# Down stages: normalized rows split in row form on GpSimd and turned by two-byte DMA transposes, in place of TensorE transposes

## The chip, the cores and the metric

The kernel runs on one core of a Trainium2 chip. The time is the device time of one execution in microseconds (us). A core has five engines that run side by side, each with an instruction queue of its own that is worked off in order: TensorE (PE in the profile, its weight loads PEld), VectorE (DVE), ScalarE (ACT), GpSimd (POOL) and SyncE (SP), which here only issues DMA transfers. An instruction starts when the one before it on its engine is through and the semaphores that it waits for are there. Matmul results go to PSUM, eight banks of 128 x 512 fp32; GpSimd doesn't read PSUM in this kernel.

## The reference, cut to what matters

The program is a macaron layer on x of 2048 tokens x 1024 features: half a feed-forward network, a state-space convolution, and half a feed-forward network again, with the same weights, each on the layer-normalized x.

```
x = x + 0.5 * ffn(layernorm(x))
x = x + s4(layernorm(x))          # convolution along the last axis
x = x + 0.5 * ffn(layernorm(x))

ffn(x): h = silu(x @ Wg) * (x @ Wu);  return h @ Wd
Wg, Wu: 1024 x 2752, Wd: 2752 x 1024
W[k, n] = (nibble(k, n) - (zero(group k, n) + 1)) * scale(group k, n)   # 4 bits, groups of 128 rows
```

All data is fp32. The change concerns `layernorm(x)` on its way into `x @ Wg` and `x @ Wu`.

## The kernel before

**Jobs.** The tokens are cut in four blocks of 512 (TB), each of four row tiles of 128 tokens (NT = 4). A feed-forward network for one block is a job, so there are eight; the list `JOBS` (L1351) gives block and kind (1: first network, 3: second). Each job has two stages. `gate_up` (the up stage, L669) runs over 64 steps: eight waves of output columns times eight groups of 128 input features. `down` (the down stage, L747) runs over 44 steps: two halves of the output features times 22 chunks of the hidden features. The last chunk of a half holds half as many matmuls.

**Precision.** The quantized weights are held as signed bytes in DRAM, and every step loads one tile of them (`load_bytes`, four steps ahead, on SP's DMA queue) and casts it to fp32r, a rounded fp32 (`make_weights`, three steps ahead, on GpSimd, L643). The other operand is split into two parts so that their sum is fp32: for the up stage xTh in fp32r and xTl, the rest, in fp16; for the down stage hh and hl (L727, L729, both made by GpSimd from hf). So each step of the down stage is 4 output chunks x 2 parts = 8 matmuls of 128 x 512. After each step ScalarE or VectorE multiplies the PSUM bank in place by a ratio of scales (L665, L667). The cast weights have five buffers (`wpool`), the bytes six (`bpool`). The cast of a step's weights therefore waits until TensorE is through with the step five before it.

**The normalized input.** The up stage needs the normalized rows transposed: features on the partitions, tokens along the free axis. xTh and xTl have one buffer each. They are free once the up stage of a job is through, and must be full when the up stage of the next job begins. So they are filled during the down stage between, while TensorE works on the down matmuls. This is done by hooks: `at(dn, step, f)` has f's instructions written at that step. For each row tile t of the next job's block (`ab`):

- at step 1 + 4t `normalized` (L218) subtracts the mean and multiplies by the reciprocal deviation on VectorE, 128 x 1024 at once (xn);
- at steps 2 + 4t and 4 + 4t `turn` (L234) handles one half of the 1024 features: four TensorE transposes of 128 x 128 into one PSUM bank (pt, L228), ScalarE's copy of it into xTh, which rounds to fp32r (L250), and VectorE's subtraction pt - xTh into xTl (L251).

Job 0's down stage is later (it starts at step 10) and takes another way with `by_pool=True`: ScalarE copies the bank to SBUF and GpSimd makes both parts (L246 to L248).

Down stages also reload x of the job's own block (`load_x`) and add the finished first output half back to it: four transposes of y per row tile (`back`, pb, L780), from step 26 on.

**Order.** A planner turns the written order into each engine's queue. It moves an instruction ahead of an earlier written one on the same engine if it takes the earlier one to be still waiting. Pools hand out buffers: `xpool` ten of 128 x 1024 fp32 (x, xn and other temporaries, by `t4`), `hfpool` and `gpool` three each of 128 x 512 fp32 (hf; silu's result g).

Of the kernel before, what the change touches and what calls it, by code (L numbers as in the profile page):

```python
# [9 lines left out]
F32 = mybir.dt.float32  # L10
BF16 = mybir.dt.bfloat16
F16 = mybir.dt.float16
# [4 lines left out]
F32R = mybir.dt.float32r  # L17
AF = mybir.ActivationFunctionType
ALU = mybir.AluOpType
# [5 lines left out]
P = 128  # L25
HID = 1024
INTER = 2752
TOK = 2048
TB = 512
NT = TB // P  # L30
NC = HID // P
# [24 lines left out]
def macaron_s4_kernel(  # L56
# [31 lines left out]
    nc = tc.nc  # L88
# [7 lines left out]
    xtpool = ctx.enter_context(tc.tile_pool(name="xT", bufs=1))  # L96
# [4 lines left out]
    gpool = ctx.enter_context(tc.tile_pool(name="g", bufs=3))  # L101
    hfpool = ctx.enter_context(tc.tile_pool(name="hf", bufs=3))
# [27 lines left out]
    def t4(name):  # L130
        return xpool.tile([P, HID], F32, tag="x", name=name)
# [9 lines left out]
    def in_order_of_writing(f, *engines):  # L141

        start = len(nc.cur_bb.bb.instructions)
        got = f()
        written = list(nc.cur_bb.bb.instructions)
        for e in engines:
            last = next((i for i in reversed(written[:start]) if i.engine == e), None)
            for ins in written[start:]:
                if ins.engine == e:
                    if last is not None:  # L150
                        tc.add_manual_dep(
                            ins,
                            last.name,
                            mybir.DependencyInfo(
                                mybir.DependencyClass.NoSync, mybir.DependencyReason.DATA
                            ),
                            reason="order of writing",
                        )
                    last = ins
        return got  # L160


    x = {}
    ln = {}

    def load_x(b, src):
        x[b] = []
        for t in range(NT):
            xt = t4(f"x_{b}_{t}")
            nc.sync.dma_start(xt, src[t])  # L170
            x[b].append(xt)

    def rows_of(dram, b):
        return [dram[bass.ds(b * TB + t * P, P), :] for t in range(NT)]

    def moments(b, k):
        for _ in moments_by_tile(b, k):
            pass

    def moments_by_tile(b, k):  # L180

        name = f"{b}_{k}"
        stats = small.tile([P, NT, 2, 6], F32, tag="stats", name=f"stats_{name}")
        mv = small.tile([P, NT, 2], F32, tag="mv", name=f"mv_{name}")
        for t in range(NT):
            for i in range(2):
                nc.vector.bn_stats(stats[:, t, i, :], x[b][t][:, bass.ts(i, 512)])  # L187
            nc.vector.bn_aggr(mv[:, t, :], stats[:, t, :, :].rearrange("p a s -> p (a s)"))
            yield
        guess(b, k, mv)  # L190
# [13 lines left out]
    def deviations(b, k, factor=1.0):  # L204


        mv, ve, r = ln.pop(b)
        e = small.tile([P, NT], F32, tag="e", name=f"e_{b}_{k}")
        for three in (3.0, 12.0, 768.0):
            nc.vector.tensor_tensor(e, r, r, ALU.mult)  # L210
            nc.vector.tensor_tensor(e, e, ve, ALU.mult)
            nc.vector.scalar_tensor_tensor(r, e, three, r, ALU.subtract, ALU.mult)
        nc.vector.tensor_scalar(r, r, -factor / 8192, None, ALU.mult)
        for t in range(NT):
            ln[b, t] = (mv[:, t, 0:1], r[:, t : t + 1], k)
        return r

    def normalized(b, t):  # L218
        m, r, k = ln[b, t]
        n = t4(f"xn_{b}_{k}_{t}")  # L220
        nc.vector.tensor_scalar(n, x[b][t], m, r, ALU.subtract, ALU.mult)
        return n

    def turned(n, name):

        ps = bank(name)
        for k in range(4):
            nc.tensor.transpose(ps[:, bass.ts(k, P)], n[:, bass.ts(k, P)], ident)  # L228
        return ps.rearrange("p (c t) -> p c t", c=4)


    pieces = {}

    def turn(b, t, n, half, by_pool=False):  # L234
        k = ln[b, t][2]
        if b not in pieces:
            pieces[b] = [
                xtpool.tile([P, NC, TB], dt, tag=f"xT{w}", name=f"xT{w}_{b}_{k}")
                for w, dt in (("h", F32R), ("l", F16))
            ]  # L240
        hi, lo = (a[:, 4 * half : 4 * half + 4, bass.ts(t, P)] for a in pieces[b])
        ps = turned(n, f"pt_{b}_{k}_{t}_{half}")
        if by_pool:
            both = gpool.tile([P, TB], F32, tag="g", name=f"turn_{b}_{k}_{t}_{half}")
            both = both.rearrange("p (c t) -> p c t", c=4)
            nc.scalar.copy(both, ps)  # L246
            nc.gpsimd.tensor_copy(hi, both)
            nc.gpsimd.tensor_tensor(lo, both, hi.bitcast(F32), ALU.subtract)  # L248
        else:
            nc.scalar.copy(hi, ps)  # L250
            nc.vector.tensor_tensor(lo, ps, hi.bitcast(F32), ALU.subtract)  # L251

# [275 lines left out]
    def in_pieces(at, hooks_and_steps, pieces):  # L530

        held = {}

        def piece(last):
            def step():
                if not held:
                    held[0] = pieces()
                for _ in held[0]:
                    if not last:
                        break  # L540

            in_order_of_writing(step, ET.DVE)

        for i, (hooks, s) in enumerate(hooks_and_steps):
            last = i == len(hooks_and_steps) - 1
            at(hooks, s, lambda last=last: piece(last))
# [114 lines left out]
    h = {}  # L661
# [128 lines left out]
    after = const.tile([P, 4, P], F32, tag="after", name="after")  # L790
# [227 lines left out]
    def s4_toeplitz():  # L1018

        rows, turn, whole = t4("s4_rows"), t4("s4_turn")[:, :P], t4("s4_whole")  # L1020
        nc.gpsimd.memset(turn, 0.0)
        nc.gpsimd.affine_select(
            out=turn,
            in_=turn,
            pattern=[[1, P]],
# [327 lines left out]
    def fast():  # L1353
        for j, (b, k) in enumerate(JOBS):
            prev = JOBS[j - 1] if j else None
            after = JOBS[j + 1] if j + 1 < len(JOBS) else None
            up, dn = {}, {}

            def at(hooks, s, f):
                hooks.setdefault(s, []).append(f)  # L1360
# [65 lines left out]
            if after:  # L1426
                ab, ak = after
                if ak == 1:
                    at(up, 55 if j == 0 else 6, lambda: load_x(ab, rows_of(u, ab)))
                    if j == 0:  # L1430
                        steps = [(dn, d) for d in range(3, 8)]
                        in_pieces(at, steps, lambda: moments_by_tile(ab, 1))
                        newton = lambda: deviations(ab, 1, LIFT)
                        at(dn, 8, lambda: in_order_of_writing(newton, ET.DVE))
                    else:
                        both = lambda: moments(ab, 1)
                        at(up, 44, lambda: in_order_of_writing(both, ET.DVE))
                        at(up, 45, lambda: deviations(ab, 1, LIFT))
                an = {}

                pool = j == 0

                def anorm(t):
                    an[t] = normalized(ab, t)

                o = 9 if j == 0 else 0
                for t in range(NT):
                    at(dn, o + 1 + 4 * t, lambda t=t: anorm(t))
                    at(dn, o + 2 + 4 * t, lambda t=t: turn(ab, t, an[t][:, :512], 0, by_pool=pool))
                    at(dn, o + 4 + 4 * t, lambda t=t: turn(ab, t, an[t][:, 512:], 1, by_pool=pool))  # L1450
# [6 lines left out]
        b = JOBS[-1][0]  # L1457
# [116 lines left out]
    srow_next, zeros_down = in_order_of_writing(start, *STARTING, ET.PE)  # L1574
    x.pop(0)
    fast()
    x.clear()
    other = nc.values_load(flag)
# [84 lines left out]
```

## Time and profile before

| what | us |
|---|---|
| median of 3 runs | 2136.39 (2135.84 to 2138.37) |
| the profiled execution | 2136.97 |
| its span, first to last instruction | 2135.1 |
| TensorE busy | 2087.0 |
| VectorE busy | 1702.1 |
| ScalarE busy | 1420.6 |
| GpSimd busy | 1072.9 |
| TensorE transposes pt (L228), 224, busy | 36.8 |
| ScalarE xTh <- pt (L250), 48 | 28.3 |
| VectorE xTl (L251), 48 | 33.1 |
| GpSimd weight casts for the down stages (L643), 352 | 222.4 |
| GpSimd waiting for TensorE before these | 338.6 |

The profile is of one execution. The span leaves out 1.9 us of its time before the first and after the last instruction. Busy times are sums over an engine's instructions. Those of TensorE overlap[...], so 128 x 128 transposes with a mean of 272 ns follow each other more closely than that; what a stretch of them takes is read from the chain in order of time. The chain is followed back from the last instruction, at each step to whatever released it. Of the 224 transposes pt 32 belong to job 0's down stage and 192 to those of jobs 1 to 6. The granted TensorE clock was 0.997 of full speed over the span.

### The profile page before, as it was taken

How to read it: one execution, taken by the hardware profiler on the slowest of the kernel's cores; microseconds unless marked ns; L12 is line 12 of the kernel's file. 1: busy time of each engine (PE TensorE's matmuls, PEld its weight loads, DVE VectorE, ACT ScalarE, POOL GpSimd, SP SyncE). 2: the span in 40 equal slices, each digit the busy share in tenths (PEclk: the TensorE clock that was granted, in tenths of full speed). 3: DMA queues.
4: the chain of work that ended last, by engine and by line, in shares of the span. 5: the costliest groups of instructions: out<-in, count | busy, mean ns of one | idle time of the engine just before them, and what ended most of it. 6: DMA issues, size and time to landing. Idle time of an engine off the chain costs nothing.

```text
span 2135.1 us, 30272 instructions
## 1 busy us (share of the span) xinstructions
PE 2087.0 (98%) x9748; PEld 1425.8 (67%) x9748; DVE 1702.1 (80%) x2781; ACT 1420.6 (67%) x2233; POOL 1072.9 (50%) x1438
## 2 busy tenths in 40 slices
PE   6999999999999999999999999999999999999997
PEld 4555665677776578665876568675686766866576
DVE  8988877778888777778777888878788787777776
ACT  6877777646655776676767766547775467767765
POOL 6867838743354643555335543455534545345632
PEclk9999999999999999999999999999999999999999
DMA  4434321112111211112121121112111131121111
GB/s 141 124 92 131 100 70 55 37 58 74 43 45 47 93 50 54 65 31 92 56 80 38 29 73 39 44 52 70 35 38 38 51 98 44 45 81 36 33 35 58
DMA packets 163110, 132.14 MB, mean 62 GB/s; under 512 B 22651, under 2 KB 150500, under 8 KB 162942
## 3 DMA queue, kind: packets, MB, share of 16 engines
q1 hardware_dynamic: 161926, 128.24, 19.7%
q8 instruction: 79, 1.29, 0.2%
q10 hardware_dynamic: 728, 1.29, 0.2%
q14 instruction: 89, 0.73, 0.1%
q0 software_dynamic: 288, 0.59, 0.1%
HBM read 104.45 MB, written 25.50 MB: 61 GB/s over the span
## 4 chain that ended last, share of the span: by engine, by line
PE 88%; DVE 6%; POOL 2%; DMA 1%; issue 1%; ACT 1%; SPq 0%; ACTq 0%; DVEq 0%; POOLq 0%
PE pg L695 53%; PE po L758 27%; PE pc L1084 3%; DVE pg L667 2%; PE pb L780 1%; PE pb L1084 1%; PE pt L228 1%; DVE po L667 1%; PE st L228 1%; DVE hf L725 1%; POOL q L551 0%; POOL qd L580 0%; POOL xTl L248 0%; DMA b<-wq 0%; POOL w_down L643 0%
## 5 line engine op out<-in xcount | busy, mean ns | idle before, releaser
L665 ACT ACTIVATE pg<-pg,rat 128x512 f32<-128x512 f32 x1240 | 787.1, 660 | 424.3 <-PE pg L695 423.2
L667 DVE TENSOR_TENSOR pg<-pg,rat 128x512 f32<-128x512 f32 x1168 | 776.9, 694 | 174.0 <-PE pg L695 170.0
L695 PE MATMUL pg<-xTh,w_up 128*128 128x512 f32 x2752 | 851.5, 438 | 2.7 <-DVE pg L667 1.7
L695 PE MATMUL pg<-xTl,w_up 128*128 128x512 f16 x2752 | 722.0, 382 | 8.5 <-POOL xTl L1518 3.2
L643 POOL CAST w_up<-b 128x768 fp32r<-128x768 int8 (+2 forms) x490 | 377.4, 776 | 519.0 <-PE pg L695 407.9
L695 PEld LDWEIGHTS pg<-xTh,w_up 128*128 128x128 f32 x2752 | 519.6, 189 | 176.8 <-DVE pg L667 14.9
L758 PE MATMUL po<-hl,w_down 128*128 128x512 f32 x1344 | 539.2, 403 | 9.5 <-DVE po L667 8.0
L665 ACT ACTIVATE po<-po,ratd 128x512 f32<-128x512 f32 x660 | 430.8, 662 | 159.0 <-PE po L758 159.0
L758 PE MATMUL po<-hh,w_down 128*128 128x512 f32 x1344 | 523.3, 392 | 0.0
L667 DVE TENSOR_TENSOR po<-po,ratd 128x512 f32<-128x512 f32 x620 | 427.4, 698 | 97.3 <-PE po L758 93.0
L695 PEld LDWEIGHTS <-w_up 128*128 128x128 bf16 x2752 | 228.1, 99 | 332.7 <-issue 156.2
L643 POOL CAST w_down<-bd 128x512 fp32r<-128x512 int8 x352 | 222.4, 634 | 410.2 <-PE po L758 338.6
L758 PEld LDWEIGHTS po<-hl,w_down 128*128 128x128 f32 x1344 | 251.9, 188 | 86.9 <-DVE po L667 21.9
L758 PEld LDWEIGHTS po<-hh,w_down 128*128 128x128 f32 x1344 | 252.8, 188 | 45.5
L729 POOL TENSOR_TENSOR hl<-hf,hh 128x512 fp32r<-128x512 f32 x168 | 220.1, 1310 | 7.9
L725 DVE SCALAR_TENSOR_TENSOR hf<-pg,rat,g 128x512 f32<-128x512 f32 x168 | 122.9, 748 | 45.5 <-ACT g L722 37.6
L722 ACT ACTIVATE g<-pg,rat 128x512 f32<-128x512 f32 x168 | 110.7, 687 | 49.2 <-PE pg L695 39.1
L727 POOL CAST hh<-hf 128x512 fp32r<-128x512 f32 x168 | 106.3, 633 | 55.5 <-PE pg L695 34.1
L187 DVE BATCH_NORM_STATS2 stats<-x 128x6 f32<-128x512 f32 x88 | 58.6, 677 | 0.5
L1114 DVE TENSOR_TENSOR x<-x,pc 128x512 f32<-128x512 f32 x32 | 22.0, 686 | 36.9 <-PE pc L1084 36.9
L1084 PEld LDWEIGHTS pc<-near,st 128*128 128x128 f32 x256 | 43.6, 190 | 7.9
L782 DVE TENSOR_TENSOR x<-x,pb 128x512 f32<-128x512 f32 x64 | 43.2, 679 | 6.2 <-PE pb L780 6.2
(210 smaller groups left out, 1049.7 us busy)
## 6 DMA issues: line engine op xcount, KB each, us to landing
b<-wq SPq DMA_DIRECT2D x319, 96.0 KB
bd<-wdq SPq DMA_DIRECT2D x336, 64.0 KB
x<-in_L_attn_u_dram SPq DMA_DIRECT2D x30, 512.0 KB
b<-wq SPq DMA_DIRECT2D x128, 64.0 KB
xs<-x SPq DMA_DIRECT2D x16, 512.0 KB
x<-xs SPq DMA_DIRECT2D x16, 512.0 KB
out_dram<-x SPq DMA_DIRECT2D x16, 512.0 KB
b<-wq SPq DMA_DIRECT2D x64, 80.0 KB
```

The costliest lines, as they stand in the source:

```text
L187: nc.vector.bn_stats(stats[:, t, i, :], x[b][t][:, bass.ts(i, 512)])
L643: nc.gpsimd.tensor_copy(t, b)
L665: nc.scalar.activation(dst, src, AF.Copy, scale=sc)
L667: nc.vector.tensor_tensor(dst, src, sc.to_broadcast([P, TB]), ALU.mult)
L695: nc.tensor.matmul(p, weights, (lo, hi)[k][:, g, :], start=(g == 0 and not done), stop=(g == GK - 1 and done), skip_group_check=True,)
L722: nc.scalar.activation(g, pg, AF.Silu, scale=rat[:, 2 * f, GK - 1 :])
L725: nc.vector.scalar_tensor_tensor(hf, pu, last, g, ALU.mult, ALU.mult)
L727: nc.gpsimd.tensor_copy(hi, hf)
L729: nc.gpsimd.tensor_tensor(lo, hf, hi.bitcast(F32), ALU.subtract)
L758: nc.tensor.matmul(ps[c], w[:, bass.ts(c, P)], part, start=(f == 0 and k == 0), stop=(f == NF - 1), skip_group_check=True,)
L782: nc.vector.tensor_tensor(part, part, ps, ALU.add)
L1084: nc.tensor.matmul(dst, lhsT, rhs, start=start, stop=stop, skip_group_check=True)
```

## The change

In the down stages of jobs 1 to 6 a new generator `turn_by_dma` takes the place of `turn`; job 0 keeps the old way, and job 7 has no job after it. Per row tile:

- VectorE normalizes in two halves of 512 columns.
- GpSimd makes, from the rows as they are, hi (xn rounded to fp32r), top (xn in bf16), mid = hi - top in bf16 and lo = xn - hi in fp16, each in two halves. top + mid stand for hi.
- SP issues three DMA transposes of 128 x 1024 two-byte elements: top and mid into one temporary (`both`, the tile named turned), lo directly into xTl.
- GpSimd adds the transposed top and mid into xTh, in two halves (`sums`).

The temporaries: xn, hi and turned are tiles of `xpool` (`t4`), top and mid of `hfpool`, lo of `gpool`. PSUM and TensorE have no part in it. The hooks advance the generator at steps 1 + 9t + d, with d = 0 for the normalization, 1 to 6 for GpSimd's pieces, 8 for the transposes, 10 and 11 for the sums. Lines behind the new function are 47 further down in the changed kernel, and 59 behind the second edit.

```diff
--- before.py
+++ after.py
@@ -249,6 +249,53 @@
         else:
             nc.scalar.copy(hi, ps)
             nc.vector.tensor_tensor(lo, ps, hi.bitcast(F32), ALU.subtract)
+
+    def turn_by_dma(b, t, after):
+
+
+
+        k = ln[b, t][2]
+        name = f"{b}_{k}_{t}"
+        if b not in pieces:
+            pieces[b] = [
+                xtpool.tile([P, NC, TB], dt, tag=f"xT{w}", name=f"xT{w}_{b}_{k}")
+                for w, dt in (("h", F32R), ("l", F16))
+            ]
+        hi_t, lo_t = (a[:, :, bass.ts(t, P)] for a in pieces[b])
+        halves = [slice(0, 512), slice(512, HID)]
+        m, r, _ = ln[b, t]
+        n = t4(f"xn_{name}")
+        for own in halves:
+            nc.vector.tensor_scalar(n[:, own], x[b][t][:, own], m, r, ALU.subtract, ALU.mult)
+        yield
+        hi = t4(f"hi_{name}").bitcast(F32R)
+        top = hfpool.tile([P, HID], BF16, tag="hf", name=f"top_{name}")
+        mid = hfpool.tile([P, HID], BF16, tag="hf", name=f"mid_{name}")
+        lo = gpool.tile([P, HID], F16, tag="g", name=f"lo_{name}")
+        for own in halves:
+            nc.gpsimd.tensor_copy(hi[:, own], n[:, own])
+            nc.gpsimd.tensor_copy(top[:, own], n[:, own])
+            yield
+            nc.gpsimd.tensor_tensor(mid[:, own], hi[:, own].bitcast(F32), top[:, own], ALU.subtract)
+            yield
+            nc.gpsimd.tensor_tensor(lo[:, own], n[:, own], hi[:, own].bitcast(F32), ALU.subtract)
+            yield
+        both = t4(f"turned_{name}").bitcast(BF16).rearrange("p (i c t) -> p i c t", i=2, c=NC)
+
+        def transposes():
+            nc.sync.dma_start(both[:, 0], top, transpose=True)
+            nc.sync.dma_start(both[:, 1], mid, transpose=True)
+            nc.sync.dma_start(lo_t, lo, transpose=True)
+
+        transposes()
+
+        def sums():
+            for half in range(2):
+                own = slice(4 * half, 4 * half + 4)
+                nc.gpsimd.tensor_tensor(hi_t[:, own], both[:, 0, own], both[:, 1, own], ALU.add)
+                yield
+
+        after.append(sums())
 
 
 
@@ -1444,7 +1491,19 @@
                     an[t] = normalized(ab, t)
 
                 o = 9 if j == 0 else 0
-                for t in range(NT):
+                turns = {}
+
+                def turning(t):
+                    if t not in turns:
+                        turns[t] = [], []
+                        turns[t] += (turn_by_dma(ab, t, turns[t][1]),)
+                    rest = turns[t][1] or turns[t][2:]
+                    next(rest[0], None)
+
+                for t in range(NT if j else 0):
+                    for d in (0, 1, 2, 3, 4, 5, 6, 8, 10, 11):
+                        at(dn, 1 + 9 * t + d, lambda t=t: turning(t))
+                for t in range(0 if j else NT):
                     at(dn, o + 1 + 4 * t, lambda t=t: anorm(t))
                     at(dn, o + 2 + 4 * t, lambda t=t: turn(ab, t, an[t][:, :512], 0, by_pool=pool))
                     at(dn, o + 4 + 4 * t, lambda t=t: turn(ab, t, an[t][:, 512:], 1, by_pool=pool))
```

## The prediction

> **What bounds the kernel now.** I read the page first: busy shares, then the chain that ended last, then the groups.
>
> ```profile
> span 2135.1 us, 30272 instructions
> PE 2087.0 (98%) x9748; PEld 1425.8 (67%) x9748; DVE 1702.1 (80%) x2781; ACT 1420.6 (67%) x2233; POOL 1072.9 (50%) x1438
> PE 88%; DVE 6%; POOL 2%; DMA 1%; issue 1%; ACT 1%; SPq 0%; ACTq 0%; DVEq 0%; POOLq 0%
> ```
>
> TensorE carries 88% of the chain; GpSimd (POOL) is busy half of the time and has only 2% of it. Next the chain in order of time, inside the down stage of job 5 (1528 to 1611 us):
>
> ```profile
> 1547.39 0.44 PE pt L228 x4
> 1547.83 3.69 PE po L758 x16
> 1551.51 0.44 PE pt L228 x4
> 1551.95 3.71 PE po L758 x16
> 1555.66 0.44 PE pt L228 x4
> 1556.10 3.69 PE po L758 x16
> 1559.79 0.44 PE pt L228 x4
> 1560.22 17.32 PE po L758 x76
> 1577.54 0.44 PE pb L780 x4
> ```
>
> TensorE never stops here. A step of the down stage is 8 matmuls, and four transposes (pt) cost 0.44 us every second step until they end; 17.32 us for 76 matmuls is 1.83 us for a step without them. Then the time of GpSimd alone, around the start of the same stage and in its middle:
>
> ```profile
> 1526.63 0.62 POOL L643 CAST w_down<-bd 128x512 fp32r<-128x512 int8 x1
> 1527.21 1.30 POOL L729 TENSOR_TENSOR hl<-hf,hh 128x512 fp32r<-128x512 f32 x1
> 1528.44 0.63 POOL L727 CAST hh<-hf 128x512 fp32r<-128x512 f32 x1
> 1529.15 1.33 POOL L729 TENSOR_TENSOR hl<-hf,hh 128x512 fp32r<-128x512 f32 x1
> ...
> 1543.36 0.61 POOL L643 CAST w_down<-bd 128x512 fp32r<-128x512 int8 x1 [1.20 <-PE po L758]
> 1545.65 0.61 POOL L643 CAST w_down<-bd 128x512 fp32r<-128x512 int8 x1 [1.68 <-PE po L758]
> ```
>
> Two things are to be seen. Back to back, a cast takes 0.58 us from start to next start (1526.63 to 1527.21) and a two-input operation 1.24 (1527.21 to 1528.44, rounded up); 0.70 where the next one needs the cast's result. And in mid-stage GpSimd does one weight cast per step and waits for TensorE the rest: by the waits, 338.6 us in the whole run for w_down. The cast of weight k waits until step k-5 has freed its buffer, so GpSimd is never more than about four steps, 4 x 1.83 - 0.6 = 6.7 us, ahead. That is all the delay that it may suffer before TensorE stops.
>
> [...]
>
> **The change, part by part.** It acts in the down stages of jobs 1 to 6, four row tiles in each.
>
> *Removed from TensorE.* 32 transposes a stage, 8 x 0.44 = 3.5 us, all on the chain: 6 x 3.5 = 21 us. This is the whole possible gain, 1%.
>
> *Removed from ScalarE and VectorE.* Eight casts of 0.59 and eight subtractions of 0.69 us a stage; eight PSUM banks. Neither engine is the bound while TensorE runs back to back, so this counts nothing. The normalization stays on VectorE, now in halves, and of its waits in the built program none is for the new GpSimd work or the new DMAs.
>
> *Added to GpSimd.* Per tile 4 casts (hi, top) and 6 two-input operations (mid, lo, and two sums): 4 x 0.58 + 6 x 1.24 = 9.8 us, 39 us a stage. GpSimd is idle about 52 of a stage's 82 us (28.8 busy from 1530 to 1612), so the volume would fit. What decides is the order in which it stands. In the built program's order on GpSimd the four tiles are not spread over steps 1 to 39, where the hooks are written, but stand between the casts of weights 4 and 24. In jobs 2, 3 and 6 (call the cast of down weight k dk) 20 one-input operations (9 of them d5 to d13) and 17 two-input ones stand from after d4 to d13: 20 x 0.58 + 17 x 1.24 = 32.7 us. d4 ends about 0.6 us after step 0 begins, so step 13 begins at 33.3 us; unhindered it would be 13 x 1.83 = 23.8. Stall: 9.5 us. From d14 to d17 only one lo (1.24) is in the way, and GpSimd is at 36.9. Then 8 one-input (4 of them d18 to d21) and 6 two-input operations follow: 4.6 + 7.4 = 12.1, d21 ends at 48.9, where step 21 is due at 33.3 + 8 x 1.83 = 47.9: 1.0 us more.
>
> *Added waits on DMA.* The two sums of a tile wait in GpSimd's queue for the transposed top and mid; behind them stand the weight casts, and TensorE waits for these. The price of a transpose (256 KB) I bound by DMAs that stand in the chain in order of time, a load of 512 KB at the start (beside others) and one of 64 KB:
>
> ```profile
> 2.42 6.08 DMA x<-in_L_attn_u_dram
> ...
> 249.98 2.07 DMA bd<-wdq
> ```
>
> They give by interpolation 3.8[...]. mid goes behind top on one queue, so I take 4.5 us from mid's end to its landing[...]. Tiles 0 to 2 have 6 us or more of other work before their sums (mid of tile 1 also waits for top of tile 0's transfer, 6 us later): nothing. The sums of tile 3 stand only d21 to d23 behind mid, 3 x 0.58 plus 1.2 us of a lo, 3.0 us: 1.5 us wait, 1.2 of it stall. Stage sum for jobs 2, 3, 6: 9.5 + 1.0 + 1.2 = 11.7.
>
> Jobs 4 and 5 have the same order, but the last sums one weight earlier, just before d23: 1.9 more, 13.6. In job 1 the first halves of hi are not done ahead, and 23 one-input and 18 two-input operations stand to d14: 35.7 + 0.6 - 14 x 1.83 = 10.7 stall; the second stretch 1.0 again; its last sums stand 1.2 us behind mid with three transfers close together, some 5 to 6 us: together 18 (17 to 19).
>
> *Added to SP.* Twelve transposes a stage, which wait there for GpSimd; a weight load's issue takes 0.32 us. Loads queued behind (bd13 behind tile 0, bd23 to bd28 behind tiles 2 and 3) are cast at least six weights, 11 us, later. Nothing; if that cover went, each microsecond would be one of the cast. DMA rings are 12 to 15% busy in the stage.
>
> *Sum.* Stalls 18 + 3 x 11.7 + 2 x 13.6 = 80.3; dependent pairs at 0.70 in place of 0.58, some four a stage, 6 x 0.5 = 3; gain 21. 80.3 + 3 - 21 = +62. The profiled execution took 2136.97 us (span 2135.1 and 1.9 around it): 2199. The median of the runs, 2136.39, is 0.6 lower, so I say 2199 for the median too.
>
> **Rivals.**
> *A, transfers decide.* With three transposes at 3 us of ring time each, the sums of all tiles come late: the same walk through the queue gives 111 us of stall, +90, 2227; at 4 us 150 and +129, 2266[...]. It decides from about 2.5 us each. For it: [...]that nothing here has transposed by DMA. Against: regular DMAs of this trace move 64 KB in 2.07.
> *B, GpSimd is lighter.* If mid and sums, with two-byte operands, took 0.75 to 0.9 us, the walk gives 42 to 51 us of stall, +21 to +30: 2158 to 2167. Against it: xTl (L248) with a two-byte result has 1.29 us in the median, no less than fp32.
> *C, faster.* GpSimd's pieces hide entirely in its 52 idle microseconds, and the 3.5 us a stage are kept: 2136 - 21 = 2115. The place is the stretch d4 to d13; it needs two-input operations of about 0.5 us or less, since even at 0.58 the walk leaves +4 to +10. For it: the idle share. Against: 168 operations of L729, none under 1.26.
>
> **How the numbers follow.** The forecast has 0.70, A from 3 us upward 0.15, B 0.10, C 0.03, and 0.02 for a draw where B meets the gain. The range reaches from B's 2158 to A's at about 4 us, 2275; what is left out is C, the lightest of B and the slowest of A, less than 2 in 10. This kernel's measurement tells 0.2%, 4 us, from no change. Faster by over that 0.04, within it 0.02, slower 0.94.
>
> **What would show it.** Right: 9556 TensorE matmuls instead of 9748; GpSimd 24 x (4 x 0.61 + 6 x 1.28) = 243 us busier, near 1316; groups of L758 waiting for POOL w_down for about 80 us, where before it was 0.8 and 2.4; the stall between steps 7 and 13 of the down stage and again at 21 to 24, none after step 25; GpSimd waiting for the transposed tile almost only at the last sums. Wrong: long waits of the sums for tiles 0 to 2 (A), two-input operations under 1 us (B), TensorE as dense in the first half of a down stage as before (C), or VectorE stopped at its normalization, which I cost at nothing.

## The result, and the profile after

| | before | after |
|---|---|---|
| median, us | 2136.11 (2134.03 to 2138.37, 4 runs) | 2202.80 (2201.39 to 2205.41, 4 runs) |
| ratio | | 1.0313, 95% interval 1.0295 to 1.0331 |
| span of the profiled execution | 2135.1 | 2200.0 |

The change costs 66.7 us, 3.1%. The forecast was 2199. First the page of the changed kernel, its span and busy line:

```profile
span 2200.0 us, 30236 instructions
PE 2092.1 (95%) x9556; PEld 1405.4 (64%) x9556; DVE 1706.6 (78%) x2757; ACT 1397.4 (64%) x2185; POOL 1292.3 (59%) x1678
```

The 192 transposes are gone (9748 to 9556 matmuls) and GpSimd is 219 us busier. Where the time went is seen from the length of the down stages, from the end of the last gate matmul to the end of the last po matmul in the timeline of TensorE (us):

| job | 1 | 2 | 3 | 4 | 5 | 6 | 7 |
|---|---|---|---|---|---|---|---|
| before | 86.0 | 85.3 | 85.2 | 85.4 | 85.3 | 85.2 | 81.4 |
| after | 99.2 | 95.9 | 95.5 | 95.7 | 95.5 | 96.1 | 81.4 |

Nearly all of it, 65.5 us, lies in the six stages with the change; job 7, which has no turns, is the same. The waits of the changed kernel's engines (us in total, times, longest):

```profile
PEld po L805 <- POOL w_down L690: 71.3, 54, 2.9
PEld po L805 <- DVE po L714: 47.5, 81, 2.2
POOL mid L279 <- DMA turned<-top: 13.6, 6, 3.0
POOL xTh L295 <- DMA turned<-mid: 12.2, 6, 2.7
```

The two waits of TensorE stood so in the kernel before:

```profile
PEld po L758 <- DVE po L667: 21.9, 44, 1.6
PEld po L758 <- POOL w_down L643: 2.4, 4, 1.2
```

TensorE now waits for down weights that GpSimd casts, and more than before for VectorE's evictions of po (its multiplications of the PSUM bank po in place). GpSimd itself waits for transfers. The time of TensorE's weight loads in job 2's down stage, which begins at 775.2; the number in brackets is the wait before the instruction:

```profile
796.29 0.19 PEld L805 LDWEIGHTS po<-hl,w_down 128*128 128x128 f32 x1 [1.67 <-POOL w_down L690]
...
802.68 0.19 PEld L805 LDWEIGHTS po<-hl,w_down 128*128 128x128 f32 x1 [2.31 <-POOL w_down L690]
809.38 0.19 PEld L805 LDWEIGHTS po<-hl,w_down 128*128 128x128 f32 x1 [1.60 <-POOL w_down L690]
813.75 0.19 PEld L805 LDWEIGHTS po<-hl,w_down 128*128 128x128 f32 x1 [2.22 <-DVE po L714]
...
827.20 0.76 PEld L805 LDWEIGHTS po<-hb,w_down 128*128 128x128 f32 x4 [1.18 <-POOL w_down L690]
833.88 0.19 PEld L805 LDWEIGHTS po<-hl,w_down 128*128 128x128 f32 x1 [2.26 <-POOL w_down L690]
```

These are steps 9, 11, 13, 14, 21 and 24; steps 8 and 10, left out, wait 0.68 each. All but step 14, which waits for VectorE, wait for a cast. There are two stretches, and nothing after. What GpSimd did meanwhile, from its timeline, beside the lines of before in which it made one cast per step and waited:

```profile
799.66 0.62 POOL L276 CAST hi<-xn 128x512 fp32r<-128x512 f32 x1
800.22 0.63 POOL L277 CAST top<-xn 128x512 bf16<-128x512 f32 x1
800.79 1.28 POOL L281 TENSOR_TENSOR lo<-xn,hi 128x512 f16<-128x512 f32 x1
802.00 0.63 POOL L690 CAST w_down<-bd 128x512 fp32r<-128x512 int8 x1
...
818.57 1.17 POOL L279 TENSOR_TENSOR mid<-hi,top 128x512 bf16<-128x512 f32 x1 [2.14 <-DMA turned<-top]
...
826.53 1.73 POOL L690 CAST w_down<-bd 128x512 fp32r<-128x512 int8 x3
831.01 2.26 POOL L295 TENSOR_TENSOR xTh<-turned 128x512 fp32r<-128x512 bf16 x2 [2.75 <-DMA turned<-mid]
833.22 3.52 POOL L690 CAST w_down<-bd 128x512 fp32r<-128x512 int8 x6
```

In the first stretch GpSimd runs without a pause (from 775.65 to 812.81), and the cast of weight 11 at 802.00 comes behind 3.4 us of pieces, a mid from 798.56 on and the three shown; TensorE, through with step 10 at 800.8, starts step 11 with the cast's end at 802.68. The last step of the stage to wait, 24, begins when the cast at 833.22 is through; that cast stood behind two sums, and these behind a transfer. The chain of waits, which in this profile can be followed back only to 1625 us, shows the same in job 6 (start, duration, work):

```profile
1867.22 1.34 POOL mid L279
1868.57 0.56 POOL w_down L690
1869.12 2.25 POOL xTh L295 x2
1871.37 0.55 POOL hi L276
1871.92 0.57 POOL w_down L690
1872.49 0.04 issue
1872.53 1.67 PE po L805 x6
```

Before, the chain ran through TensorE for a whole stage; here it goes through GpSimd's queue until a cast lets TensorE make one step.

### The profile page after: what moved, and what is told of

Same layout as the page of the kernel before. It is cut to its first block, busy times and chain, and to the rows that moved or that the text cites. A ratio compares the mean times of both kernels' runs of the same rounds, so it can differ in the third digit from the quotient of the medians.

```text
span 2200.0 us, 30236 instructions
## 1 busy us (share of the span) xinstructions
PE 2092.1 (95%) x9556; PEld 1405.4 (64%) x9556; DVE 1706.6 (78%) x2757; ACT 1397.4 (64%) x2185; POOL 1292.3 (59%) x1678
## 3 DMA queue, kind: packets, MB, share of 16 engines
q1 hardware_dynamic: 237958, 147.12, 24.3%
## 5 line engine op out<-in xcount | busy, mean ns | idle before, releaser
L279 POOL TENSOR_TENSOR mid<-hi,top 128x512 bf16<-128x512 f32 x48 | 58.1, 1211 | 13.6 <-DMA turned<-top 13.6
L281 POOL TENSOR_TENSOR lo<-xn,hi 128x512 f16<-128x512 f32 x48 | 62.7, 1307 | 0.0
L295 POOL TENSOR_TENSOR xTh<-turned 128x512 fp32r<-128x512 bf16 x48 | 54.8, 1163 | 12.2 <-DMA turned<-mid 12.2
```

The lines of the kernel that those rows point to most:

```text
L279: nc.gpsimd.tensor_tensor(mid[:, own], hi[:, own].bitcast(F32), top[:, own], ALU.subtract)
L281: nc.gpsimd.tensor_tensor(lo[:, own], n[:, own], hi[:, own].bitcast(F32), ALU.subtract)
```

## The experiments

Three explanations were to be told apart. *Theory 1*: the order on GpSimd; casts are late because pieces are crowded ahead of them. *Theory 2*: the DMA transposes, by their landing or by their place in SP's queue. *Theory 3*: VectorE, one of whose normalizations lasts 3.5 to 4.9 us in each stage. Medians are of four or more runs. The kernel before, measured beside each group, stayed between 2135.98 and 2136.46, so medians of different groups are compared.

### The pieces where the hooks write them

```diff
-                    next(rest[0], None)
+                    in_order_of_writing(lambda: next(rest[0], None), ET.Pool)
```

> The whole computation of the changed kernel, with one difference: the GpSimd pieces keep the places by weight at which the hooks write them (one or two pieces after each cast from d5 to d42) instead of being pulled together between d4 and d24. Theory 1, the order on GpSimd makes the weight casts late: at most some 2 pieces (1.3 to 1.9 us) stand between two casts, so TensorE's waits for w_down fall from 120 us to under 15, VectorE's long normalization half goes too, [...]and the time is 2115 to 2130. Theory 2, the DMA transposes (landing, and their place in SP's queue) decide: the sums still stand two or three steps behind the transposes, GpSimd waits for them there in all four tiles, and the time stays above 2180.

Measured: 2122.43 us, ratio to before 0.9936 (0.9919 to 0.9952); below this is called the spread order. The order alone takes away 80.4 us and makes the change a gain of 0.6%. Stages of jobs 1 to 6: 85.0, 83.2, 83.1, 83.2, 83.1, 83.1. The waits:

```profile
PEld po L805 <- DVE po L714: 39.9, 91, 1.8
PEld po L805 <- POOL w_down L690: 2.5, 4, 1.2
PE po L805 <- POOL w_down L690: 0.8, 1, 0.8
```

Waits for w_down are those of the kernel before again. GpSimd has as much to do (1289.6 us busy), and none of its operations waits for a transposed tile, because the sums stand far behind: in the stretch below mid's transpose is issued at 790.42 and the sum stands at 796.40.

```profile
790.04 0.61 POOL L690 CAST w_down<-bd 128x512 fp32r<-128x512 int8 x1
790.61 1.30 POOL L281 TENSOR_TENSOR lo<-xn,hi 128x512 f16<-128x512 f32 x1
791.85 1.17 POOL L690 CAST w_down<-bd 128x512 fp32r<-128x512 int8 x2
...
795.82 0.62 POOL L690 CAST w_down<-bd 128x512 fp32r<-128x512 int8 x1 [1.25 <-issue]
796.40 1.16 POOL L295 TENSOR_TENSOR xTh<-turned 128x512 fp32r<-128x512 bf16 x1
```

There is a piece or two between casts, and there are pauses in GpSimd's timeline again: it is ahead. The stop is a matter of order and not of volume. But the spreading also keeps sums away from their transfers, so this run alone doesn't part theory 1 from theory 2.

### No transposes, the order left to the planner

```diff
-            nc.sync.dma_start(both[:, 0], top, transpose=True)
-            nc.sync.dma_start(both[:, 1], mid, transpose=True)
-            nc.sync.dma_start(lo_t, lo, transpose=True)
+            pass
```

(lo is written into lo_t by its operation, and the sums read top and mid.)

> Leaves out the transposition by DMA in jobs 1 to 6: the sums read top and mid in row form and lo is written straight into the tile it would be turned into, so that the projection gets rows that were not turned. GpSimd's operations are the same in number, and the planner still pulls them together, now between d4 and d15. Theory 1 (GpSimd's order): with the same 40 pieces in fewer weights the casts are as late or later, the time stays above 2180. Theory 2 (transfers and SP's queue decide): 75 us of stalls go with the transfers, and the time is 2115 to 2130. If the stall is GpSimd's but the transfers' part is what I put at 1.2 us a stage, the stages' lengths change by no more than 2 us.

Measured: 2211.62 us, ratio 1.0351 (1.0333 to 1.0368), 8.8 us slower than with the transposes. Without a single transfer to wait for, the planner crowds the same pieces between d4 and d15, and TensorE waits as before for w_down (57.0 us on its weight loads, 71.3 in the changed kernel). The run also has a stop that the changed kernel doesn't have. In five stages VectorE's normalization waits for GpSimd's lo (the tile xTl in this run):

```profile
DVE xn L269 <- POOL xTl L281: 20.3, 5, 4.1
```

TensorE then waits for VectorE's po, up to 4.6 us at once. So the size of this loss can't be put down to late casts alone, but it is a loss without any transfer: transfers aren't needed for one. How much of it they make in the changed kernel's own order is left to a pair below.

### Normalization on ScalarE

```diff
+        bias = small.tile([P, 1], F32, tag="nbias", name=f"nb_{name}")
+        nc.vector.scalar_tensor_tensor(bias, m, -1.0, r, ALU.mult, ALU.mult)
...
-            nc.vector.tensor_scalar(n[:, own], x[b][t][:, own], m, r, ALU.subtract, ALU.mult)
+            nc.scalar.activation(n[:, own], x[b][t][:, own], AF.Identity, bias=bias, scale=r)
```

> The whole computation; the normalization of jobs 1 to 6 is done by ScalarE (scale and bias) in place of VectorE, GpSimd's pieces and the transposes are those of the changed kernel. After the change one normalization half in each stage lasts 3.5 to 4.9 us on VectorE while GpSimd runs without a gap, and the po evictions behind it make TensorE wait (38 us more waiting for VectorE's po). Theory 3, this starved VectorE carries a part of the loss: the time falls by 13 to 38 us, to 2165 to 2190. Theory 1 alone (the weight casts are late by themselves, and the waits for po lie in the same time): within 5 us of the changed kernel, 2198 to 2205.[...]

Measured: 2201.21 us, ratio 1.0312 (1.0292 to 1.0332): no difference to the changed kernel. So the loss doesn't need VectorE's long normalization, and theory 3 falls as its main cause. The instructions of xn, min/median/max ns, first those of this run, then VectorE's in the changed kernel:

```profile
L271 ACT ACTIVATE xn<-x,nb,r x48: 801/810/822, 488.4 to 1889.0; 128x512 f32<-128x512 f32 x48
```

```profile
L269 DVE TENSOR_SCALAR xn<-x,mv,r x48: 530/642/4869, 489.0 to 1889.9; 128x512 f32<-128x512 f32 x48
```

On ScalarE the operation always takes 0.81 us. The wait for VectorE became shorter (PEld for DVE's po 47.5 to 30.0), and the wait for w_down grew (71.3 to 81.3). But the planner crowded the pieces a little more in this run (in job 2 the 26 pieces of the first stretch stand ahead of a cast one weight earlier), so the run doesn't measure what the long normalization adds by itself.

### The gain alone

```diff
-        ps = turned(n, f"pt_{b}_{k}_{t}_{half}")
+        ps = turned(n, f"pt_{b}_{k}_{t}_{half}") if by_pool else n.rearrange("p (c t) -> p c t", c=4)
```

This edit is made in the kernel before.

> The kernel before, without TensorE's 192 transposes in the down stages of jobs 1 to 6: the copies of ScalarE and VectorE read the normalized rows as they are, so the transposition is left out. It measures the gain alone. By the chain the transposes cost 6 x 8 x 0.44 = 21 us: 2115. If they were covered by waits, less: 2115 to 2136.

Measured: 2127.99 us, ratio 0.9962 (0.9950 to 0.9975), 8.0 us less than the kernel before beside it and not 21. Stages are 83.7 to 84.5 us, 1.5 us shorter where 3.5 were expected. Waits of TensorE in this run:

```profile
PEld po L758 <- DVE po L667: 30.3, 59, 2.1
PEld po L758 <- ACT po L665: 10.5, 38, 0.8
PEld po L758 <- POOL w_down L643: 8.3, 19, 1.1
```

They were 21.9, 4.1 and 2.4 before. The waits for VectorE's and ScalarE's work on po grew by 14.8 us together, those for casts by 5.9. The reading is that VectorE and ScalarE emptied accumulators, and GpSimd cast weights, while TensorE made its transposes; with the transposes gone TensorE comes back sooner, and waits. No run tells the three apart.

### A pair: one order on GpSimd, with and without transposes

In both, the pieces stand nearly where the changed kernel has them in jobs 2, 3 and 6 (ahead of some casts stands a piece less, and two casts to hi stand inside the stage instead of ahead of it; call it the held order), and the casts of weights 5 to 29 are held in the written order too:

```diff
+                AS_AFTER = (
+                    (0, 1, 2, 2, 2, 3, 3, 5, 5, 5),
+                    (1, 4, 4, 4, 6, 7, 7, 9, 9, 9),
+                    (4, 7, 8, 8, 8, 9, 10, 16, 16, 16),
+                    (8, 14, 15, 15, 16, 17, 17, 20, 20, 20),
+                )
...
-                    for d in (0, 1, 2, 3, 4, 5, 6, 8, 10, 11):
-                        at(dn, 1 + 9 * t + d, lambda t=t: turning(t))
+                    for d in AS_AFTER[t]:
+                        at(dn, d, lambda t=t: turning(t))
```

> The whole computation of the changed kernel; its GpSimd order of jobs 2, 3 and 6 (pieces from d4 to d13 and d17 to d23) is written out by hand for all of jobs 1 to 6 and held there, the weight casts with it. It is the pair of the next run. Theory 1 (the order on GpSimd): down stages of 95 to 98 us as in the changed kernel, the whole 2195 to 2210; that shows at once that this order, and not something else that the planner moved, makes the time.

> The same GpSimd order, operation for operation, with the transposition by DMA left out: no transposes are issued, the sums read top twice in row form, lo is written in rows into the tile that it would be turned into. So nothing on GpSimd waits for a transfer, and no transpose stands in SP's queue before or behind the weight loads. Theory 1: only what the transfers add goes, by my forecast the wait at the last sums (1.2 us a stage), 7 us in all: 2188 to 2200. Theory 2 (the transposes' landing and their place in SP's queue carry the loss): stages near 84 us, the whole below 2135. A difference of 15 to 40 us between the pair would put a middle part on the transfers.

Measured: 2245.72 us with transposes (1.0516, 1.0498 to 1.0533), 2178.58 without (1.0196, 1.0179 to 1.0213). Both expectations of theory 1 were missed, one upward, one downward. The first run's waits tell why:

```profile
POOL mid L279 <- DMA turned<-top: 56.3, 18, 4.2
POOL xTh L295 <- DMA turned<-mid: 3.7, 6, 0.9
```

A mid waits for a buffer that it shares with earlier tops: three such buffers, held until the transpose of the top is through. Here 18 of them wait, 6 in the changed kernel, because SP's queue came out in another order. Its timeline (start, time at issue):

```profile
793.83 1.26 SPq L288 DMA_TRANSPOSE xTl<-lo  x1
795.18 0.54 SPq L681 DMA_DIRECT2D bd<-wdq  x1
795.77 1.23 SPq L286 DMA_TRANSPOSE turned<-top  x1
```

Tile 0's top was made by 790.5, but its transpose stands behind that of lo. In the changed kernel the same transpose was issued at 784.80, less than 0.1 us after top was made. So the first of the pair isn't quite the changed kernel, and the pair has more to say on transfers than on it: 60.0 us of waits on GpSimd (56.3 + 3.7) go with 67.1 us of time, 1.12 us for each. And the second of the pair, the crowded order with no transfer in it, is 56.2 us above the spread order (2178.58 - 2122.43), 24.2 below the changed kernel, which waits 25.8 us for transfers on GpSimd (13.6 + 12.2). As an estimate, then, about 56 of the changed kernel's 80.4 us of stops are pieces crowded ahead of casts. The other 24 are mainly waits for transfers in the same queue, but not surely all: the changed kernel's matmuls of po also wait 20.7 us for VectorE, against 12.9 and 12.7 in the pair, where no normalization lasts over 1.5 us.

### Four weight buffers

```diff
-    wpool = ctx.enter_context(tc.tile_pool(name="w", bufs=5))
+    wpool = ctx.enter_context(tc.tile_pool(name="w", bufs=4))
```

In the changed kernel:

> The whole computation of the changed kernel with four buffers for converted weights in place of five; the order on GpSimd is the same, one weight earlier. Theory 1: a cast may be late by what the buffers cover, four steps before, three now. The same pieces then stall TensorE by 1.83 us more in each stage if the cover counts once (stages +1.8, the whole +11, 2214), by up to 3.7 us more if it counts again at the second stretch (the whole +22, 2225). If the loss isn't a matter of that cover (if TensorE waited for the transposed tile or for VectorE by themselves), no change: 2200 to 2206.

In the one with the pieces as written:

> The whole computation; GpSimd's pieces where the hooks write them, and four weight buffers. It is the control of the run before: no more than 1.9 us of pieces stand between two casts, so three steps of cover (5.5 us less a cast) are enough: within 4 us of the same order with five buffers, 2119 to 2127. If four buffers hurt the gate and up stages, which have no pieces, this run shows by how much, and the run before has to be read against it.

And in the changed kernel with `bufs=4` for the pool hf as well:

> The whole computation; the changed kernel with four weight buffers, and a fourth buffer for top and mid (room that the fifth weight buffer leaves). GpSimd's order is that of the run with four weight buffers but for one exchange of mid and lo of tile 3. A mid that had to wait for the transfer of the tile's earlier top (13.6 us in six waits in the changed kernel) finds a buffer free. Theory 1 with a transfers' part: those waits go, and with them 8 to 14 us against the run with four weight buffers. If waits on GpSimd that stand behind a transfer cost nothing: within 4 us of it.

Measured: 2218.15 us (1.0380, 1.0363 to 1.0398), 2131.52 (0.9979, 0.9972 to 0.9986) and 2211.71 (1.0351, 1.0333 to 1.0368). The control missed its expectation: four buffers cost 9.1 us also where the pieces are spread. So of the changed kernel's 15.4 us more, 6.3 are left for the crowded order by the medians, 1.0 a stage. By the lengths of the stages in the profiled executions the six stages grew by 14.8 us where the pieces are crowded and by 4.2 where they are spread, which leaves 1.8 a stage, about the 1.83 of a whole lost step. TensorE's wait for w_down on its weight loads grew from 71.3 to 104.3 us in the crowded order, from 2.5 to 4.9 in the spread one. The sign is as the cover asks. The size isn't settled, also because VectorE's long normalization is gone in this run (the longest lasts 1.51 us).

The fourth buffer of hf took all 13.6 us of the mids' waits away, and the sums waited more, 17.5 us for 12.7: 8.8 us fewer on GpSimd, and 6.4 us less time, 0.73 for each, below the 8 to 14 expected. With the 1.12 of the pair this gives a second estimate of the transfers' part in the changed kernel: 25.8 us times 0.73 to 1.12, 19 to 29 us.

### Versions that beat both

The pieces as written, and the normalization on ScalarE:

> The whole computation; GpSimd's pieces where the hooks write them, and the normalization of jobs 1 to 6 on ScalarE. With the pieces spread, stages take 83.5 us against 81.7 for job 7, which has no turns, and the TensorE waits that are longer in them are those for VectorE's evictions of po (4.7 us on its weight loads in job 3, 2.1 in job 7). If VectorE's normalization, 8 x 0.8 us a stage, is what delays them, the stages fall to 82 and the time by 6 to 11 us, to 2111 to 2117. If ScalarE's evictions are delayed as much in their place, it stays at 2119 to 2126.

Measured: 2120.78 us, ratio 0.9929 (0.9913 to 0.9946), stages 82.4 to 83.2. The lowest time of all, but its interval overlaps that of the spread order alone, and most of the 6 to 11 us hoped for didn't come. TensorE's wait for VectorE's po fell from 39.9 to 29.1 on weight loads.

The pieces as written, and the casts to hi and top on ScalarE:

```diff
-            nc.gpsimd.tensor_copy(hi[:, own], n[:, own])
-            nc.gpsimd.tensor_copy(top[:, own], n[:, own])
+            nc.scalar.copy(hi[:, own], n[:, own])
+            nc.scalar.copy(top[:, own], n[:, own])
```

> The whole computation; GpSimd's pieces where the hooks write them, but the casts to hi and top done by ScalarE (16 a stage, 0.6 us each) instead of GpSimd. If GpSimd's order is harmless once it is spread, as theory 1 says, lifting 10 us a stage from GpSimd gains nothing: 2119 to 2126. If the GpSimd load itself still costs, [...]3 to 8 us less. If ScalarE's evictions become late, more: 2126 to 2140.

Measured: 2128.06 us, ratio 0.9964 (0.9951 to 0.9976), 5.6 us more than the spread order alone, 2 us outside the first expectation and in the third. GpSimd has 52 us less to do and nothing is won; TensorE's wait for ScalarE's po rose from 4.7 to 11.3 us. In this order, in which GpSimd is ahead, its work costs nothing, and ScalarE's does.

## Why the forecast was right, and where its terms were off

The forecast was 2199, +62 from its base; +66.7 was measured. The mechanism is the one forecast, casts made late by the order on GpSimd. That the number came within 4 us is in part luck: errors of 7 to 11 us of either sign stand in its terms. Point by point:

- **GpSimd's order** ("What decides is the order in which it stands"). Shown: the order alone moves 80.4 us, at equal work. The steps that stop are those named, 7 to 13 and 21 to 24: in job 2 a cast is late at 8 to 11, 13, 21 and 24. TensorE's weight loads wait 71.3 us for casts, forecast about 80.
- **Sum of the stops**, forecast 83 (80.3 and 3 for dependent pairs), measured 80.4 as the difference to the spread order. By stage, after minus spread: 14.2, 12.7, 12.4, 12.5, 12.4, 13.0 for jobs 1 to 6, forecast 18, 11.7, 11.7, 13.6, 13.6, 11.7 before the pairs. The sum agrees better than its two parts. From crowded pieces the working has 10.7 + 1.0 in job 1, 10.5 in each other stage, and the 3, together 67; the runs show about 56, by the estimate above. From transfers it has 16 (6.3 in job 1, 1.2 in jobs 2, 3 and 6, 3.1 in 4 and 5); the runs show about 24.
- **Pieces 11 too many.** Mid and the sums, with two-byte operands, are a little lighter than taken: from start to start mostly 1.10 to 1.12 us in the timeline (a sum or mid to what follows it) against 1.24, which was read from hl and which the author took for all of them as an estimate. The 96 of them make 11 to 13 us in the six stages. That is rival B's direction, but a tenth and not a third.
- **Transfers 8 too few: the term "Added to SP ... Nothing".** The forecast looked only at weight loads behind transposes. The reverse counted: transposes behind weight loads that wait for casts, which stand behind the pieces. In the changed kernel's job 2 GpSimd was through with tile 3's mid at 825.35, but SP (start, time at issue) was still at two loads, the second of which was issued at 827.17, when the cast at 826.53 was through:

```profile
824.24 3.25 SPq L681 DMA_DIRECT2D bd<-wdq  x2
827.54 1.24 SPq L287 DMA_TRANSPOSE turned<-mid  x1
```

  and the sums began at 831.01. From the start of the issue to the sums 3.5 us, less than the author's estimate of 4.5, but 2.2 us in the queue came ahead of it. The other half of the transfers' waits is the first mid of tile 3, in each of the six stages, waiting for the buffer of tile 2's top. In job 2 that top was made by 804.86, and its transpose was issued 9 us later, behind six weight loads, which waited in turn for casts:

```profile
813.98 1.26 SPq L286 DMA_TRANSPOSE turned<-top  x1
```

  The forecast named a wait of this kind for tile 1's mid alone and put it at nothing. It looked for long waits for transposed tiles "almost only at the last sums", and the sums of the first tiles indeed don't wait.
- **The gain, 21 us, "all on the chain", was the worst term.** The kernel before without its transposes shows 8.0. The step that failed is the sentence on ScalarE and VectorE, "Neither engine is the bound while TensorE runs back to back": with the transposes out, TensorE waits 14.8 us more for their work on po. Where the change also takes ScalarE's copies and VectorE's subtractions away and the pieces stand spread on GpSimd, the gain is 13.7 us (the spread order against before); that these two account for the difference to 8.0 wasn't tested. Set against that, the forecast's +62 is 80.4 - 13.7 = +66.7: the error of the gain, 7.3, less that of the stops, 2.6.
- **VectorE at its normalization** was costed at nothing. It stopped for up to 4.9 us and TensorE waited for it. Without it there is still a loss: in the run with ScalarE (2201 us) and in the held order without transposes (42 us above before), where no normalization lasts over 1.4 us. What it adds in the changed kernel's own order stays open.
- **Rival A** (transfers decide) is excluded: a crowded order without transfers is still 42 us slower than before, and a spread one with them is faster. **Rival C** (hidden entirely, 2115) is close to what the pieces give when they stand as written: 2122. It needed the order, not the lighter operations that the forecast asked of it.

## What to carry to other kernels

Idle time of an engine is worth something only at the places where work is put (here 80.4 us lie between two orders of the same work): before adding work to an engine that feeds TensorE, read from the built order how much of it stands ahead of each feeding instruction, and compare that with the lead that its buffers allow. An in-order DMA queue can close a circle, as it did here: loads waiting for casts hold up the transposes for which those casts' engine will wait (25.8 us in the changed kernel). And a transpose's time on TensorE's chain isn't its worth: 21 us of them brought 8.0 alone, because TensorE then waited longer for what came next, here mostly the work on its accumulators (14.8 us more). A run with the work left out measures that at once.

## What the runs showed of the hardware that was not expected

**TensorE at half clock after a stop.** Stretches of 1 us in the changed kernel around the stop at 802.68 (columns: stretch, us, busy time and instructions of PE, PEld, DVE, ACT and POOL, granted clock, DMA share, GB/s):

```profile
802.00:803.00 1.00, 0.32 (x1) 0.30 (x2) 0.00 (x0) 0.00 (x0) 1.00 (x3) 1.00 2.17 38
...
805.00:806.00 1.00, 1.00 (x4) 0.77 (x3) 0.08 (x1) 0.66 (x1) 1.00 (x2) 0.50 0.83 328
...
807.00:808.00 1.00, 1.00 (x6) 0.64 (x4) 0.68 (x1) 0.73 (x2) 1.00 (x2) 1.00 0.99 225
```

Matmuls follow each other every 0.43 us instead of 0.23 for about 3 us. Counted over the matmuls of po in the timeline, this happened 4 times in the changed kernel (about 5 us more), 13 times in the held order with transposes (17 to 19 us), 3 times in the held order without (about 5 us), 8 times in the run without transposes whose order the planner chose (12 us), never in the kernel before or in the spread order. In the changed kernel stops in which TensorE was idle 1.77 to 1.91 us came before it, while others as long had no such effect: after the stops of 2.51 us before 548.36 and of 1.84 before 833.88 the granted clock stayed at 1.00. What decides between the two wasn't found. Such a stop costs more than itself, and some 12 to 14 of the 67.1 us between the pair are of this kind: without them the pair has 0.9 us of time for each us of wait.

**VectorE held up beside GpSimd.** In the changed kernel's job 2, from the timelines of VectorE and of GpSimd:

```profile
808.85 4.24 DVE L269 TENSOR_SCALAR xn<-x,mv,r 128x512 f32<-128x512 f32 x1
813.01 0.68 DVE L714 TENSOR_TENSOR po<-po,ratd 128x512 f32<-128x512 f32 x1
```

```profile
808.71 0.62 POOL L690 CAST w_down<-bd 128x512 fp32r<-128x512 int8 x1
809.28 1.30 POOL L281 TENSOR_TENSOR lo<-xn,hi 128x512 f16<-128x512 f32 x1
810.51 2.30 POOL L690 CAST w_down<-bd 128x512 fp32r<-128x512 int8 x4
```

The normalization, 0.53 us at its shortest (L269), lasts here until these six GpSimd instructions are through. That it waits for them isn't shown beyond this coincidence: one such case stands in each stage (3.5 to 4.9 us), and in the held order, with GpSimd as crowded, the same operation never took over 1.5 us. On ScalarE it took 0.82 at most. What makes the one place so bad wasn't tried.

**A DMA transpose in SP's queue** took 1.24 to 1.31 us to issue (medians of L286, L287 and L288 in the changed kernel, 24 each), where a load of down weights took 0.32 (median of L681). On the rings the 72 transposes of 256 KB took 1.5 to 1.6 us of all 16 engines each, by the share of queue q1: it rose from 19.7% of 2135.1 us to 24.3% of 2200.0, 114 us, against the run without transposes (19.4% of 2209.1) 106.
